# A Mamba block's weights for the scan prepared two steps earlier, and the next block's time-step work moved behind the first block's convolutions

## The chip, the cores and the metric

The kernel runs on one core of a Trainium2 chip. Its time is the device time of one launch in microseconds; a row of times comes from repeated launches, and one more launch is recorded by the hardware profiler. A core has a matrix engine (TensorE, PE in the profile), a vector engine (VectorE, DVE), a scalar engine (ScalarE, ACT) and GpSimd (POOL); SyncE (SP) issues most of the transfers. Each engine works through its own queue of instructions strictly in order, and a queue stands still while its first instruction waits for another engine.

## The reference

Four layers follow one another on an input of 2 x 1024 tokens of 512 features, each as `x = layernorm(x + layer(x))`: a Mamba-2 layer, a ternary linear layer, an RG-LRU layer and a gated feed-forward layer with integer weights. The change touches only the first. Cut to what matters:

```python
zxbcdt = hidden_states @ W_in                 # gate 1024 | x 1024, B 16, C 16 | dt 16
xBC = silu(causal_conv4(zxbcdt[..., 1024:2080]) + conv_b)
dt = softplus(zxbcdt[..., 2080:] + dt_bias)   # one per head, 16 heads of 64
dA = exp(dt * -exp(A_log))
# over the tokens t:
h = h * dA_t + (dt_t * x_t) outer B_t
y_t = h @ C_t
# then
y = (y + D_skip * x) * silu(gate)
y = y * rsqrt(mean(y * y) + 1e-5) * norm_w
out = y @ W_out
```

## The kernel before, in words

The 2048 tokens are worked on in four blocks (b = 0 to 3) of 512; two blocks make one sequence. Inside a block the recurrence over tokens is done in four chunks (c) of 128 tokens: the part inside a chunk is a product with a 128 x 128 matrix of weights for each head, and only the state H goes from chunk to chunk.

`head(b)` transposes the block's tokens (L219), multiplies them with the B, C and time-step columns of W_in (L340), convolves B and C (the taps at L251, 32 rows, silu at L299), and works out softplus and decays. For block 0 this is done on 128 partitions. For the others it is done in `by_rows`, on 64 rows of 128 tokens: L427 adds the bias, `softplus` (L195 to L206) follows, then L429 to L431, an exponential on ScalarE (L432), a cumulative product (L433), and two writes to DRAM (`since`, L436, and `decays`, L438). After a `yield` one transpose on TensorE (L442) and a copy (L443) bring the time steps and B into the layout `tk` by token.

`project(b)` runs for blocks 1 to 3. Four transfers (L546) broadcast the decays to all partitions of the tile L, 16 heads of 512 tokens, four heads each. Then eight steps m follow. `inner(m)` is a product of four matmuls into one PSUM bank (px, L323), a copy to SBUF (xpad, L458), the scaled start of the convolution (acc, L293), three taps on VectorE (L251) and a silu (xc, L299). `grams` makes the products of B and C (pgm, L474, copied to gm at L480). `scans(h0)` copies four heads of L into PSUM (pl, one bank each, L516) and makes running products of them on VectorE (L522). `weigh(h0)` makes bdec on VectorE (L532) and multiplies the four heads by gm on GpSimd (L537). `spans` fetches the decay since the start of a chunk (cdec, L493), with a small copy on VectorE (over, L505) and a product on GpSimd (L506). At the end `by_token` transposes the first chunk (pxt, L619) and scales it by the time steps (dtx, L621).

Between these steps `weave` puts pieces of `conclude(b - 1)`, the output product of the block before (po, L715, one bank for each of four groups of 128 tokens; the row sums pss, L724; the update of x, L730), by a plan that says after which step how many pieces come:

```python
            fill, plan = conclude(b - 1, before), (0, 0, 2, 0, 2, 0, 2, 2)
```

`recur(b)` is the recurrence: products py (L642 with the state, L650 within the chunk), the new state (pst, L660; L667, L674), the sum into xc (L681), and the next chunk's `by_token`. Between its chunks come pieces of `gates` (the gate's columns of W_in, pg, L323, silu at L692) and of the next block's `head`. Then `gate` multiplies by the gate on VectorE (L700), squares on ScalarE (L702) and adds up on GpSimd (L704).

Block 0 has no block before it. Its projection is written out in `opening`, where TensorE, VectorE and ScalarE keep the written order (`manual_schedule`); the convolutions there read PSUM (L306, taps L312, silu L316). Its last two lines before the remaining convolutions call the next block's head twice:

```python
        next(coming)
        for conv in later:
            next(g)
            conv()
```

The recurrence of block 0 then has the head of block 1 (`ahead`) and the gate (`g`) in turns:

```python
            turns = (ahead, g, g, ahead, g, g)
            weave(recur(b, H, st), (next(steps, None) for steps in turns), (2, 2, 1, 1))
```

Outside `opening` a planner that simulates the engines sets the order of the instructions in each queue; the program's order and its dependencies are what it starts from. `keep_in_program_order` pins an instruction to its place. The PSUM pool `ps` has eight banks with one tag, and all products share them in turn: a product must wait until the reader of an earlier tile in its bank is done.

Of the kernel before, what the change touches and what calls it, by code (L numbers as in the profile page):

```python
# [13 lines left out]
ALU = mybir.AluOpType  # L14
# [8 lines left out]
NX = DI // P  # L23
# [14 lines left out]
def model_kernel(ctx: ExitStack, tc: tile.TileContext, t: dict, out: bass.AP):  # L38
    nc = tc.nc
    ctx.enter_context(nc.allow_non_contiguous_dma(reason="small parameter columns"))  # L40
    BATCH, SEQ, _ = t["L0_attn_hidden_states"].shape
# [68 lines left out]
    by_hj = cp.tile([HJ, 5], F32, tag="by_hj", name="by_hj")  # L110
# [134 lines left out]
                x[:, j, :], x[:, j, :], mv[:, j, 0:1], rs[:, j, :], ALU.subtract, ALU.mult  # L245
            )

    def causal_conv(acc, xpad, w):

        for k in range(3):  # L250
            nc.vector.scalar_tensor_tensor(  # L251
                acc, xpad[:, k : k + TB], w[:, k : k + 1], acc, ALU.mult, ALU.add
            )

    def weave(main, fill, plan, rest=True):

# [29 lines left out]
    def started(pm, n, b, row, w, bias, dst, xpad):  # L286

        if b % BPS == 0:
            nc.gpsimd.memset(xpad[:n, 0:3], 0.0)
        else:  # L290
            nc.gpsimd.tensor_copy(xpad[:n, 0:3], carry[:n, row, :])
        acc = tmp("acc")
        nc.scalar.activation(acc[:n, :], pm[:n, :], AF.Identity, bias=bias, scale=w[:, 3:4])  # L293
        if b % BPS < BPS - 1:
            nc.gpsimd.tensor_copy(carry[:n, row, :], xpad[:n, TB : TB + 3])

        def rest():
            causal_conv(acc[:n, :], xpad[:n, :], w)
            nc.scalar.activation(dst, acc[:n, :], AF.Silu)  # L299

        return rest
# [27 lines left out]
    def head(b, st):  # L329

        if b >= 3:
            X.append(tokens())
            nc.sync.dma_start(X[b], xin[b])
        xT = st["xT"] = transposed(mp, b, X, bufs=2, by_act=b > 0)[0]

        pm = bank("pbc")
        half = TB // 2
        for k in range(NK):
            for i in range(2):
                nc.tensor.matmul(  # L340
                    pm[i * 64 : i * 64 + NR, :half], w_in[:, k, 2 * DI : IN_DIM],
                    xT[:, k, i * half : (i + 1) * half], start=(k == 0), stop=(k == NK - 1),
                )
        rows = mp.tile([P, 3 + TB], F32, tag="xpad", name="rpad", bufs=3)
        for i in range(2):
            nc.scalar.copy(
                rows[:NR, 3 + i * half : 3 + (i + 1) * half], pm[i * 64 : i * 64 + NR, :half]
            )
        BC = st["BC"] = mp.tile([NBC, TB], F32, tag="BC", name="BC")

        mix = started(rows[:, 3:], NBC, b, NX, cwr, cbr, BC, rows)
        tk = sp.tile([P, 2, NJ, NH], F32, tag="tk", name="tk")
        dt, bt = st["dt"], st["bt"] = tk[:, 0], tk[:, 1]
        if b:

            turn = mp.tile([P, P], F32, tag="a2", name="turn")
            nc.sync.dma_start(
                turn[:HJ], rows[32:NR, 3:].rearrange("h (j t) -> h j t", t=P)
            )
        if b < 2:  # L360
            yield
        if b:
            mix()
            nc.sync.dma_start(turn[HJ:], BC[:NS].rearrange("n (j t) -> n j t", t=P))
            nc.sync.dma_start(crow[b], BC[NS:])
            st["CT"] = mp.tile([P, TB], F32, tag="rows", name="CT", bufs=2)
            nc.sync.dma_start(st["CT"], crow[b].unsqueeze(0).to_broadcast([8, NS, TB]))
            yield
            yield from by_rows(b, turn, tk)
            return  # L370

        z = sp.tile([P, NJ, NH], F32, tag="z", name="z", bufs=1)
        a = sp.tile([P, NJ, NH], F32, tag="a", name="a", bufs=1)
        pdt = bank("pdt")
        for j in range(NJ):
            nc.tensor.transpose(
                pdt[:, j * NH : (j + 1) * NH], rows[32:NR, 3 + j * P : 3 + (j + 1) * P],
                ident[32:NR, 32:NR],
            )
        nc.vector.tensor_tensor(  # L380
            z, pdt[:, : NJ * NH].rearrange("p (j h) -> p j h", h=NH),
            dtb.unsqueeze(1).to_broadcast([P, NJ, NH]), ALU.add,
        )
        softplus(dt.rearrange("p j h -> p (j h)"), z.rearrange("p j h -> p (j h)"), NJ * NH)
        nc.vector.tensor_tensor(a, dt, rootA.unsqueeze(1).to_broadcast([P, NJ, NH]), ALU.mult)
        nc.vector.scalar_tensor_tensor(
            a, a, 1.0e18, rootN.unsqueeze(1).to_broadcast([P, NJ, NH]), ALU.min, ALU.mult
        )
        nc.vector.tensor_tensor(a, a, endless.unsqueeze(1).to_broadcast([P, NJ, NH]), ALU.min)
        for lo in (0, 32):  # L390
            nc.vector.tensor_scalar(a2[:, :, lo : lo + NH], a, LOG_FLOOR, None, ALU.max)
        yield
        pa = bank("pa")
        for j in range(NJ):
            nc.tensor.transpose(pa[:NR, j * P : (j + 1) * P], a2[:, j, :], ident)
        dA, cum = tmp("dA")[:NR], tmp("cum")[:NR]
        nc.scalar.activation(dA, pa[:NR, :], AF.Exp)

        r = st["r"] = mp.tile([NR, TB], F32R, tag="rows", name="rows", bufs=2)
        nc.scalar.activation(r, pa[:NR, :], AF.Exp)  # L400
        yield
        nc.vector.tensor_tensor(r[32:NR], dA[32:NR], r[32:NR].bitcast(F32), ALU.subtract)
        nc.vector.memset(r.bitcast(F32).rearrange("r (j t) -> r j t", t=P)[:, :, 0:1], 0.0)
        mix()
        yield
        for j in range(NJ):
            w = slice(j * P, (j + 1) * P)
            nc.vector.tensor_tensor_scan(
                cum[:, w], dA[:, w], zeros[:NR].to_broadcast([NR, P]), 1.0, ALU.mult, ALU.add
            )  # L410
        rc = st["rc"] = mp.tile([NR, TB], F32R, tag="rows", name="rows", bufs=2)
        nc.scalar.copy(rc, cum)
        yield
        nc.vector.tensor_tensor(rc[32:NR], cum[32:NR], rc[32:NR].bitcast(F32), ALU.subtract)
        yield

    def by_rows(b, turn, tk):


        z, work = turn[:HJ], [tmp(f"work{i}")[:HJ] for i in range(2)]  # L420
        e, r, s, s2, p, a, dA, cum = (
            w[:, i : i + P] for w in work for i in range(0, TB, P)
        )
        if b == 1:
            exponents(*(by_hj[:, i : i + 1] for i in range(1, 5)))
        bias, _, end, rA, rN = (by_hj[:, i : i + 1] for i in range(5))
        nc.vector.tensor_scalar(z, z, bias, None, ALU.add)  # L427
        softplus(z, z, P, (e, r, s, s2, p))
        nc.vector.tensor_scalar(a, z, rA, 1.0e18, ALU.mult, ALU.min)  # L429
        nc.vector.tensor_scalar(a, a, rN, end, ALU.mult, ALU.min)  # L430
        nc.vector.tensor_scalar(a, a, LOG_FLOOR, None, ALU.max)  # L431
        nc.scalar.activation(dA, a, AF.Exp)  # L432
        nc.vector.tensor_tensor_scan(  # L433
            cum, dA, zeros[:HJ].to_broadcast([HJ, P]), 1.0, ALU.mult, ALU.add
        )
        nc.sync.dma_start(since[b].rearrange("h (j t) -> (h j) t", t=P), cum)  # L436
        nc.vector.memset(dA[:, 0:1], 0.0)
        nc.sync.dma_start(decays[b].rearrange("h (j t) -> (h j) t", t=P), dA)  # L438
        yield

        pt = bank("ptk")
        nc.tensor.transpose(pt[:, :P], turn, ident)  # L442
        nc.vector.tensor_copy(tk, pt[:, :P].rearrange("p (v n j) -> p v j n", v=2, j=NJ))  # L443
        yield
# [96 lines left out]
    def project(b, st):  # L541

        inner, crows, grams, spans, scans, weigh = parts(b, st)

        for h0 in range(0, NH, 4):
            nc.sync.dma_start(  # L546
                L[:, h0 : h0 + 4, :].rearrange("p h t -> p (h t)"),
                decays[b, h0 : h0 + 4].rearrange("h t -> (h t)").partition_broadcast(P),
            )
        inner(0)()  # L550
        yield
        inner(1)()
        yield
        grams()
        inner(2)()
        yield
        for m in range(3, NX):
            inner(m)()
            if m == 6:
                spans()  # L560
            if m < 7:
                scans(4 * m - 12)
                weigh(4 * m - 12)
            yield
        st["dtx"] = by_token(st, 0)
        yield

    def opening(st, own, g, coming):
# [32 lines left out]
        later.pop(0)()  # L601
        later.append(inner(7))
        later.pop(0)()
        next(coming)
        for conv in later:
            next(g)
            conv()
# [140 lines left out]
    for b in range(NBLK):  # L748
# [5 lines left out]

            weave(recur(b, H, st), alternate(itertools.chain(fill, g), ahead), (3,) * NJ)
        else:
            turns = (ahead, g, g, ahead, g, g)
            weave(recur(b, H, st), (next(steps, None) for steps in turns), (2, 2, 1, 1))
            for m in range(NX):
                tc.keep_in_program_order(nc.gpsimd.tensor_scalar(  # L760
                    w_out[:, m, :], w_out[:, m, :], normw[:, m : m + 1], 1.0, ALU.mult, ALU.mult
# [492 lines left out]
```

## Time and profile before

| what | value |
|---|---|
| median of 3 runs | 1148.89 us (1146.79 to 1148.9) |
| time of the profiled execution | 1149.05 us |
| its span on the core | 1147.2 us |
| mean granted TensorE clock | 0.994 |
| TensorE / VectorE / ScalarE / GpSimd busy | 98% / 59% / 40% / 32% |
| block 0, projection | to about 72 us |
| block 0, recurrence | 72 to 106 us |
| blocks 1, 2, 3: projection starts | 106, 214, 319 us |
| last of block 3's recurrence | about 413 us |

The span runs from the first to the last instruction of the profiled execution, and lies 1.85 us under that execution's own time. Busy shares are means over the whole span, and the stages have different limits; so what a stage is worth is read from the waits inside it. A row of the timeline gives start, length, engine, line and tiles, and in brackets the idle time before it and what released it. A row of the waits gives who waited for whom, the sum in us, the count and the longest. In rows of windows each engine has its busy time, then comes the clock granted to TensorE (1.00 is full).

### The profile page before, as it was taken

To read this page: it belongs to the slowest core of one execution; us is meant where nothing else is said; L and a number is where in the kernel's file an instruction comes from. 1 tells how busy PE (TensorE), PEld (TensorE's weight loads), DVE (VectorE), ACT (ScalarE), POOL (GpSimd) and SP (SyncE) were. 2 spreads that over 40 slices of the span, in tenths; PEclk is the share of its full clock that TensorE was granted. 3 is DMA by queue.
4 is the path that set the end of the run, shared out by engine and by line. 5 is a ranking of instruction groups with operands and counts; after the bars stand their busy time and mean duration, and the time that the engine had idled before them with its cause. 6 is when DMAs were issued, how large, how long until landed. Compare 5 with 4: busy or idle time off the path is not lost.

```text
span 1147.2 us, 12259 instructions
## 1 busy us (share of the span) xinstructions
PE 1118.7 (98%) x4614; PEld 684.2 (60%) x4614; DVE 678.9 (59%) x1228; ACT 459.0 (40%) x700; POOL 361.9 (32%) x347
## 2 busy tenths in 40 slices
PE   8989999999999999999999999999999999999995
PEld 5455445445544555654444444448888888888884
DVE  4887896696769676863717237083328765225224
ACT  3343544463454233566654372533223223223222
POOL 1446472555248240556123212237401001001002
PEclk9999999999999999999999999999999999999998
DMA  8004002400220038112000000004501001001001
GB/s 316 20 14 167 2 1 89 166 0 37 69 113 0 38 144 234 74 31 89 1 1 0 1 0 1 0 1 128 175 1 38 1 1 37 1 1 37 1 1 40
DMA packets 32699, 59.22 MB, mean 52 GB/s; under 512 B 11808, under 2 KB 12608, under 8 KB 30072
## 3 DMA queue, kind: packets, MB, share of 16 engines
q1 hardware_dynamic: 31608, 58.21, 14.5%
q8 instruction: 38, 0.62, 0.2%
q14 instruction: 29, 0.24, 0.1%
q10 hardware_dynamic: 864, 0.14, 0.1%
q0 software_dynamic: 160, 0.01, 0.0%
HBM read 49.47 MB, written 8.68 MB: 51 GB/s over the span
## 4 chain that ended last, share of the span: by engine, by line
PE 84%; DVE 10%; ACT 4%; issue 1%; POOL 0%; DVEq 0%; ACTq 0%; POOLq 0%
PE pgu L1098 21%; PE p L947 17%; PE po L1121 10%; PE pg L323 9%; PE px L323 7%; PE po L715 6%; PE po L1024 4%; PE py L650 3%; DVE acc L251 2%; PE po L896 2%; DVE L L522 2%; PE pxt L619 1%; PE pt L219 1%; DVE xc L700 1%; PE py L642 1%
## 5 line engine op out<-in xcount | busy, mean ns | idle before, releaser
L1107 DVE SCALAR_TENSOR_TENSOR h<-pgu,L_ffn_up_scale,sg 128x512 f32<-128x512 f32 x64 | 47.9, 749 | 147.7 <-PE pgu L1098 143.7
L323 PE MATMUL px<-xT,w_in 128*128 128x512 f32 x256 | 114.6, 597 | 0.2 <-DVE over L509 0.2
L537 POOL TENSOR_TENSOR L<-L,gm 128x512 f32<-128x512 f32 x64 | 93.5, 1490 | 67.0 <-DVE bdec L532 29.4
L715 PE MATMUL po<-w_out,xc 128*128 128x512 f32 x256 | 112.5, 593 | 2.1 <-DVE L L522 2.1
L947 PE MATMUL p<-xT,w 128*128 128x512 f32 x256 | 112.1, 592 | 1.4 <-ACT xT L228 1.4
L323 PE MATMUL pg<-xT,w_in 128*128 128x512 f32 x256 | 113.4, 594 | 0.0
L947 PE MATMUL p<-cv,w 128*128 128x512 f32 x256 | 111.0, 592 | 0.0
L1121 PE MATMUL po<-wd,hh 128*128 128x512 f32 x256 | 101.3, 396 | 0.0
L1098 PE MATMUL pgu<-wF__4424,wg 128*128 128x512 f32 x256 | 101.2, 396 | 0.0
L1121 PE MATMUL po<-wd,hl 128*128 128x512 f32 x256 | 101.0, 394 | 0.0
L1098 PE MATMUL pgu<-lo__4425,wg 128*128 128x512 f32 x256 | 100.7, 393 | 0.0
L1098 PE MATMUL pgu<-lo__4425,wu 128*128 128x512 f32 x256 | 100.7, 393 | 0.0
L1098 PE MATMUL pgu<-wF__4424,wu 128*128 128x512 f32 x256 | 100.7, 393 | 0.0
L1105 ACT ACTIVATE sg<-pgu,L_ffn_gate_scale 128x512 f32<-128x512 f32 x64 | 44.0, 688 | 133.1 <-PE pgu L1098 133.0
L1113 ACT CAST hh<-h 128x512 fp32r<-128x512 f32 x64 | 39.7, 621 | 117.5 <-DVE h L1107 117.3
L715 PEld LDWEIGHTS po<-w_out,xc 128*128 128x128 f32 x256 | 48.4, 190 | 63.1 <-issue 55.7
L947 PEld LDWEIGHTS p<-cv,w 128*128 128x128 f32 x256 | 48.4, 190 | 59.8 <-issue 58.6
L947 PEld LDWEIGHTS p<-xT,w 128*128 128x128 f32 x256 | 48.4, 190 | 58.8 <-issue 55.3
L323 PEld LDWEIGHTS px<-xT,w_in 128*128 128x128 f32 x256 | 47.6, 190 | 57.8 <-issue 56.3
L1195 POOL TENSOR_TENSOR x<-x,r 128x512 f32<-128x512 f32 x12 | 15.2, 1294 | 205.9 <-DVE r L1194 205.9
L323 PEld LDWEIGHTS pg<-xT,w_in 128*128 128x128 f32 x256 | 47.4, 190 | 54.3 <-issue 53.7
L251 DVE SCALAR_TENSOR_TENSOR acc<-xpad,cols,acc 128x512 f32<-128x512 f32 x72 | 67.4, 939 | 18.5 <-ACT acc L293 14.8
(268 smaller groups left out, 1937.2 us busy)
## 6 DMA issues: line engine op xcount, KB each, us to landing
L<-decays SPq DMA_DIRECT2D x12, 1024.0 KB, 9.1
x_mid<-x SPq DMA_DIRECT2D x4, 1024.0 KB, 3.8
x<-x_mid SPq DMA_DIRECT2D x4, 1024.0 KB, 6.8
st<-in_L_ffn_gate_w_dram SPq DMA_DIRECT2D x8, 512.0 KB, 4.5
st<-in_L_ffn_up_w_dram SPq DMA_DIRECT2D x8, 512.0 KB, 4.1
st<-in_L_ffn_down_w_dram SPq DMA_DIRECT2D x8, 512.0 KB, 3.6
x<-_attn_hidden_states_dram SPq DMA_DIRECT2D x3, 1024.0 KB, 9.9
out_dram<-x SPq DMA_DIRECT2D x3, 1024.0 KB, 4.4
```

Of the source, the lines that this page charges most:

```text
L251: nc.vector.scalar_tensor_tensor(acc, xpad[:, k : k + TB], w[:, k : k + 1], acc, ALU.mult, ALU.add)
L323: nc.tensor.matmul(pm[:n, :], w_in[:, k, lo : lo + n], xT[:, k, :], start=(k == 0), stop=(k == NK - 1),)
L537: nc.gpsimd.tensor_tensor(L[:, h, :], L[:, h, :], st["gm"], ALU.mult)
L650: nc.tensor.matmul(pys[i][hh * HD : (hh + 1) * HD, q, :], dtx[q][:, 2 * i + hh, :], L[:, h, s], start=(first and q == 0), stop=(q == 1), s ...
L715: nc.tensor.matmul(po, xc[:, m, j * P : (j + 1) * P], w_out[:, m, :], start=(m == 0), stop=(m == NX - 1),)
L947: nc.tensor.matmul(pm, w1[:, i, k, m * P : (m + 1) * P], rhs[:, k, :], start=(k == 0), stop=(k == NK - 1),)
L1024: nc.tensor.matmul(po, y[:, k, j * P : (j + 1) * P], w1[:, 4, k, :], start=(k == 0), stop=(k == NK - 1),)
L1098: nc.tensor.matmul(pm, w[g][:, k, cols], x[:, k, :], start=(k == 0 and x is pieces[0]), stop=(k == NK - 1 and x is pieces[-1]),)
L1105: nc.scalar.activation(sg, pgu[0], AF.Silu, scale=gs[:, m : m + 1])
L1107: nc.vector.scalar_tensor_tensor(h, pgu[1], us[:, m : m + 1], sg, ALU.mult, ALU.mult)
L1113: nc.scalar.copy(hh, h)
L1121: nc.tensor.matmul(po[j], x[:, j * P : (j + 1) * P], wd[m // GK][:, m % GK, :], start=(m == 0 and x is h[0]), stop=(m == NF - 1 and x is h ...
```

## The change

In `project`, the steps for blocks 1 to 3: `grams` stands right behind `inner(0)` (before: behind `inner(1)`), `scans` and `weigh` of the four groups of heads stand at steps 1 to 4 (before: 3 to 6), and `spans` at step 5 (before: 6). The output product's pieces keep their places in the plan.

In `opening`, the second call of the next block's head is gone, so that the convolution of block 1's B and C comes in the recurrence of block 0. The turns of that recurrence are now head, gate, head, gate, gate, gate, head, with two pieces behind the first two chunks, one behind the third and two behind the last. Two instructions are pinned for block 1: the first of the three taps of B and C, and the addition of the bias that starts the softplus, which now also stands ahead of `exponents`.

```diff
-    def causal_conv(acc, xpad, w):
+    def causal_conv(acc, xpad, w, pinned=False):
 
         for k in range(3):
-            nc.vector.scalar_tensor_tensor(
+            tap = nc.vector.scalar_tensor_tensor(
                 acc, xpad[:, k : k + TB], w[:, k : k + 1], acc, ALU.mult, ALU.add
             )
+            if pinned and k == 0:
+                tc.keep_in_program_order(tap)
...
-        def rest():
-            causal_conv(acc[:n, :], xpad[:n, :], w)
+        def rest(pinned=False):
+            causal_conv(acc[:n, :], xpad[:n, :], w, pinned)
             nc.scalar.activation(dst, acc[:n, :], AF.Silu)
...
-            mix()
+
+            mix(b == 1)
...
+        bias, _, end, rA, rN = (by_hj[:, i : i + 1] for i in range(5))
+        shifted = nc.vector.tensor_scalar(z, z, bias, None, ALU.add)
         if b == 1:
+
+            tc.keep_in_program_order(shifted)
             exponents(*(by_hj[:, i : i + 1] for i in range(1, 5)))
-        bias, _, end, rA, rN = (by_hj[:, i : i + 1] for i in range(5))
-        nc.vector.tensor_scalar(z, z, bias, None, ALU.add)
...
         inner(0)()
+        grams()
         yield
-        inner(1)()
-        yield
-        grams()
-        inner(2)()
-        yield
-        for m in range(3, NX):
+        for m in range(1, NX):
             inner(m)()
-            if m == 6:
+            if m == 5:
                 spans()
-            if m < 7:
-                scans(4 * m - 12)
-                weigh(4 * m - 12)
+            if m < 5:
+                scans(4 * m - 4)
+                weigh(4 * m - 4)
             yield
...
-        next(coming)
         for conv in later:
             next(g)
...
-            turns = (ahead, g, g, ahead, g, g)
-            weave(recur(b, H, st), (next(steps, None) for steps in turns), (2, 2, 1, 1))
+            turns = (ahead, g, ahead, g, g, g, ahead)
+            weave(recur(b, H, st), (next(steps, None) for steps in turns), (2, 2, 1, 2))
```

## The prediction

> **What bounds the kernel now.** I read the page's first part, then TensorE's waits between 50 and 425 us (the Mamba layer, the only part that the diff touches), its clock, and the order of time on VectorE and TensorE in the blocks.
>
> ```profile
> PE 1118.7 (98%) x4614; PEld 684.2 (60%) x4614; DVE 678.9 (59%) x1228; ACT 459.0 (40%) x700; POOL 361.9 (32%) x347
> ```
>
> TensorE is busy 98% of the span. A busy TensorE is no proof of its peak, but it means that time is won or lost only where TensorE stands still or runs at a lower clock. The list of waits, as waiting line, released by, us in total, times, longest:
>
> ```profile
> PE pxt L619 <- ACT xc L316: 2.4, 1, 2.4
> PE po L715 <- DVE L L522: 2.1, 2, 1.1
> PE py L650 <- issue: 0.8, 2, 0.6
> PE pxt L619 <- ACT xc L299: 0.7, 1, 0.7
> PE pt L219 <- DVE L L522: 0.5, 1, 0.5
> ```
>
> So the layer holds 6.5 us of standing still. The first wait also has an after-effect; here is TensorE's clock behind it (time, then busy of each engine, then the granted clock):
>
> ```profile
> 71.50:72.50 1.00, 0.98 (x8) 0.69 (x6) 1.00 (x3) 0.60 (x1) 0.20 (x1) 1.00 0.15 33
> ...
> 76.00:77.00 1.00, 1.00 (x12) 1.00 (x9) 0.73 (x2) 0.00 (x0) 0.37 (x1) 0.50 0.00 0
> ```
>
> The reader is to see 0.50: from about 75.5 to 78.8 us the clock is halved. Here is what it costs (start, length, TensorE's pieces of block 0's first and second chunk):
>
> ```profile
> 75.18 3.41 PE L650 MATMUL py<-L,dtx 128*64 128x128 f32 x32
> 78.52 0.84 PE L660 MATMUL pst<-dtx,bdec 128*32 128x128 f32 x16
> ...
> 84.40 1.97 PE L650 MATMUL py<-L,dtx 128*64 128x128 f32 x32
> 86.30 0.65 PE L660 MATMUL pst<-dtx,bdec 128*32 128x128 f32 x16
> ```
>
> The same work takes 1.44 + 0.19 us more the first time; with the transposes between, 1.7 us. Last, VectorE and TensorE in block 2, where the change has its second place:
>
> ```profile
> 219.33 3.57 DVE L251 SCALAR_TENSOR_TENSOR acc<-xpad,cols,acc 128x512 f32<-128x512 f32 x3 [1.91 <-ACT acc L293]
> ...
> 224.39 2.33 DVE L251 SCALAR_TENSOR_TENSOR acc<-xpad,cols,acc 128x512 f32<-128x512 f32 x3 [1.41 <-POOL cdec L506]
> ...
> 232.15 1.22 DVE L522 TENSOR_TENSOR_SCAN L<-pl,id 128x512 f32<-128x512 f32 x1 [1.18 <-ACT pl L516]
> ```
>
> ```profile
> 225.23 7.03 PE L715 MATMUL po<-w_out,xc 128*128 128x512 f32 x16
> ...
> 239.86 1.45 PE L715 MATMUL po<-w_out,xc 128*128 128x512 f32 x3
> ```
>
> VectorE has idle time early in a projection stage and scans late; TensorE reaches the first output product (po, j = 0) at 225.23 and the second at 239.86 without a wait. Blocks 2 and 3 have next to nothing to win.
>
> **The change, part by part.** No instruction is added or removed; by the built orders everything is moved, and PSUM banks, taken in program order, go to other pairs of tiles.
>
> (a) *Block 0's end.* Taken out of VectorE's queue ahead of the last convolution: three 32-row taps (L251), L427, L195, L197, L198, L199. ScalarE no longer puts two table loads (1.28 each) and two activations there. From 65.17 two convolutions of three L312 taps at 0.67 to 0.76 = 2 x 2.14 end at 69.45 (before: 74.07). ScalarE's silu of the last one then stands behind the gate's silu, which waits for TensorE and ends at 72.35; so it ends at 72.98, not 74.87. The last transpose moves from 74.92 to 73.03: **1.9 us**. The clock: TensorE did only transposes and waiting from 71.55 to 75.18, and the drop follows at 75.5; now that stretch is 71.55 to 73.3. The Trainium skill (TensorE: Matmul & The Clock Gate, Part 1) puts the drop behind an idle free-running window of about 3.4 us, and Part 4 says that transposes don't count as busy the same way; 3.6 us agrees with that, 1.75 stays below it. I take the clock as kept: **1.7 us**. Sum 3.6.
>
> (b) *Where that work goes.* The three taps go behind the second chunk's dtx, where VectorE waits for TensorE: free. The chain from L427 to the first L203 (3.1 us in block 2: 189.73 to 192.84) starts behind the last dtx of chunk 2, near 87.0, so the first L203 ends at 90.4. Then five more L203, L204, L206, L429 (0.3 each) alternate with the L681, L667, L674 and L621 of that chunk. The last L621 (dtx) ends at 96.3 to 97.1, TensorE wants it at 96.35: between 0 and 0.8, I take **0.4 lost**. Queued behind the decay's exponential and L433 and L437 are block 0's last L681 and the whole gate: they start at 98.2 (100.46 before), so VectorE gains 2.25 where TensorE gains 3.2. SyncE's loads of L wait for the decays, written at about 99 and landed 1.8 later; issued at 101.3, the first lands 5.5 to 6.3 behind that (what blocks 3 and 2 show), about 107, which ScalarE asks for at 113.5: hidden. What is left of the transposed tk (L442, L443) costs 0.2 and 0.15.
>
> (c) *Scans at steps 1 to 4: what is late next.* In the new order the first po waits for the bank of the **third scan**, and the second po for that of the **eleventh**. Behind them TensorE's whole in-order queue waits.
> Block 1: the gate, at VectorE's own pace (113.18 - 2.26 + 0.15), ends at 111.1. As before 1.9 us of ScalarE follow to the first tap (sq, xpad, acc): 113.0. Two taps beside GpSimd at 1.34 and 1.0 (1.34 and 1.65 before): 115.35. Scan, tap, scan, scan = 1.14 + 0.65 + 2 x 1.14: 119.4. TensorE gets there at 102.55 + 0.2 + px 3.43 + pgm 1.08 + px, px 6.87 = 114.1. Wait: **5.3 us**, where before there was none.
> Block 2: taps from 219.33 to 222.1, plus 4.07 gives 226.2; TensorE wants 225.2 (pgm only trades places with px): **1.0**. Block 3: taps 323.73 to 326.73, 330.85 against 330.4: **0.5**.
> From the third scan to the eleventh VectorE has 8 scans x 1.14, 6 taps x 0.65, 2 bdec x 0.33, over and reciprocal 0.15 each, L730 0.72 = 14.7, and waits 0.8 for ScalarE (a silu 0.63 stands ahead of the copy to pl, 0.55) and 0.4 for the rms behind its table load (a 0.35 of that kind is in the trace at 129.79): 15.9. TensorE needs 14.6 (225.23 to 239.86). So each second po waits **1.3**, in three blocks.
> What block 1 waits for now goes: 1.05 + 1.01 (po) and 0.65 (pxt): the last taps come at 160.7 to 163, po ends at 166: **2.7 won**.
>
> (d) *Clock in the new gap.* By the row alone (a gap of 2.44 us with transposes was enough) 5.3 us of standing still drops the clock surely: 1.7. By the skill's rule a free-running window of 3.4 must lie wholly inside: (5.3 - 3.4)/3.4 = 56%, so 0.95. I take **1.0**, ends 0 and 1.7.
>
> Sum: -3.6 + 0.4 - 2.7 = -5.9; block 1 5.3 + 1.3 + 1.0, block 2 1.0 + 1.3, block 3 0.5 + 1.3 = +11.7. Net **+5.8 us**. The profiled execution took 1149.05 (span 1147.2), the median of the runs shown is 1148.89, the same but for 0.2; so 1149.05 + 5.8 = 1154.85, against the median 1154.7. Everything behind the first layer keeps its order and shifts as a whole.
>
> **Rivals.**
> *The scans keep up (other side).* Place: block 1's first po. If its third scan ended by 114.1, and the second po and blocks 2 and 3 waited for nothing, the 5.9 won would stand: 1143.0. It decides at 11.7 new us falling under 5.9 - 2.3. For it: before, VectorE idles 1.8 + 1.5 + 1.9 + 1.2 us between 113 and 130, room that the scans could fill. Against: the 1.9 of ScalarE, two taps and three scans are 8.3 us in sequence behind the gate, and TensorE arrives 3 us behind it.
> *About no change.* The clock holds, taps run alone at 0.65 to 0.73 (1.0 less before each first po), and each second po waits 0.3: losses 4.3 + 0.3, 0 + 0.3, 0 + 0.3 against 5.9: 0.7 under the median, 1148.2. For it: the scan, which reads PSUM, kept 1.2 us everywhere. Against: the taps at 115 and 324 us, in the same place, took 1.34 and 1.5.
> *GpSimd takes VectorE's time.* Its weighing (L537, 1.26 to 1.8 each) now begins while taps of one convolution follow each other; beside GpSimd a tap took 1.34 to 1.65. Six taps per block at +0.5 make each second po 3 us later: 5.8 + 9 gives 1164. Against: alternating with scans (135 to 142 us) taps took 0.72 with GpSimd busy.
> *It does not do what it says*: ScalarE's gate silu holds the last xc, and the first wait and half clock stay: 1154.7 + 3.6 less what block 1's wait shrinks by, nothing or up to 3.6: 1155 to 1158.
>
> **How the numbers follow.** A measurement of this kernel tells 0.2% (2.3 us) from no change. Chances: forecast 0.62 (1151.5 to 1158.5, by the ends: 4 us lower if no clock drop, no dtx stall and one second po in time, 4 us higher if the taps or L674 are slowed), the scans keep up 0.06, about no change 0.14, GpSimd 0.08, no effect at block 0 0.10. Faster 0.07 (the scans keep up, a corner of the next); same 0.13; slower 0.80. For 8 in 10 the range leaves out 1143 and the tail of 1164: 1149 to 1159.
>
> **What would show it.** Right: no wait of pxt on L316 above 0.8 and no 0.50 clock near 76 us; po waiting for L522 six times, the longest about 5 us near 114, three near 1.3; no pxt wait on L299. Wrong: the first po starting within 1 us of px's end in block 1, or po waiting for something other than a scan. If po waits for more than 2 us in blocks 2 and 3 each, taps beside GpSimd were dearer than I took them. A half clock behind the long gap shows (d).

## The result, and the profile after

The changed kernel takes 1153.59 us (median of 6 runs, 1152.64 to 1156.67), the kernel before 1148.57 us beside it (6 runs, 1146.52 to 1150.29). The ratio is 1.0047, with a 95% interval of 1.0031 to 1.0063: slower by half a per cent. The profiled execution took 1153.5 us with a span of 1151.3 us; before it was 1149.05 and 1147.2.

The page's first part for the changed kernel has nearly the same busy time on TensorE, VectorE 8 us less, GpSimd 3 us more:

```profile
PE 1119.2 (97%) x4614; PEld 682.1 (59%) x4614; DVE 671.1 (58%) x1228; ACT 458.8 (40%) x700; POOL 364.6 (32%) x347
```

TensorE's waits in the Mamba layer of the changed kernel (waiting line, released by, us in total, times, longest):

```profile
PE po L715 <- DVE L L527: 4.4, 5, 1.1
PE po L715 <- POOL sums L704: 2.1, 1, 2.1
PE py L650 <- issue: 1.0, 3, 0.6
PE py L650 <- DVE dtx L621: 1.0, 2, 0.8
PE pt L219 <- DVE L L527: 0.5, 1, 0.5
PE pxt L619 <- ACT xc L318: 0.4, 1, 0.4
```

The 2.4 us of pxt behind the silu (now L318) have become 0.4, and the 0.7 us behind L299 are gone. In their place po waits six times, 6.5 us together, where it waited twice for 2.1. The second row names GpSimd's sums, which ended at the same moment; by the program's dependencies this po waits for the bank that the third scan (L527) reads, and only the pss behind it needs the sums. The times agree: each of the six po's starts 0.10 to 0.15 us after the end of a third or an eleventh scan.

The six waits, one by one, in the timeline of TensorE (the bracket is the idle time ahead):

```profile
118.82 1.53 PE L715 MATMUL po<-w_out,xc 128*128 128x512 f32 x3 [2.14 <-POOL sums L704]
...
134.77 5.82 PE L715 MATMUL po<-w_out,xc 128*128 128x512 f32 x13 [1.08 <-DVE L L527]
...
226.05 4.53 PE L715 MATMUL po<-w_out,xc 128*128 128x512 f32 x10 [0.88 <-DVE L L527]
...
241.96 7.11 PE L715 MATMUL po<-w_out,xc 128*128 128x512 f32 x16 [1.04 <-DVE L L527]
...
333.11 7.10 PE L715 MATMUL po<-w_out,xc 128*128 128x512 f32 x16 [0.40 <-DVE L L527]
...
349.01 1.53 PE L715 MATMUL po<-w_out,xc 128*128 128x512 f32 x3 [1.04 <-DVE L L527]
```

They stand at the first and the second po of each block. In the later two blocks nothing was won that could pay for them.

TensorE's first and second chunk of block 0, to be set against the 3.41 and 0.84 of before:

```profile
74.52 2.26 PE L650 MATMUL py<-L,dtx 128*64 128x128 f32 x32
76.71 0.65 PE L660 MATMUL pst<-dtx,bdec 128*32 128x128 f32 x16
...
82.40 1.97 PE L650 MATMUL py<-L,dtx 128*64 128x128 f32 x32
84.30 0.64 PE L660 MATMUL pst<-dtx,bdec 128*32 128x128 f32 x16
```

The half clock at 76 us is gone. Another one is in this execution, earlier, in work that the change doesn't touch (39.4 to 42.8 us). Windows of 4 us (time, then busy of each engine, then the granted clock):

```profile
36.00:40.00 4.00, 4.00 (x21) 2.48 (x19) 2.58 (x8) 1.93 (x4) 0.00 (x0) 0.92 0.00 0
40.00:44.00 4.00, 4.00 (x7) 1.75 (x7) 3.93 (x6) 0.63 (x1) 3.63 (x3) 0.65 0.00 0
...
76.00:80.00 4.00, 4.00 (x42) 2.67 (x38) 3.85 (x8) 0.00 (x0) 1.98 (x2) 1.00 0.00 0
```

It costs 1.34 us: block 0's last px starts that much later than before. How far the changed kernel is behind the other at some points of TensorE's queue (start after minus start before, us) shows where the time went:

| point | behind by | step |
|---|---|---|
| last px of block 0 | +1.34 | +1.34, half clock near 40 us |
| py of chunk 0 | -0.66 | -2.00, pxt's wait |
| first pxt behind it | -2.01 | -1.35, full clock in py and pst |
| pg of chunk 3 | -0.87 | +1.14, wait for dtx |
| first px of block 1 | -0.77 | +0.10 |
| first po of block 1 | +1.54 | +2.31, third scan |
| second po | +1.65 | +0.11, 1.08 in place of 1.05 |
| third po | +0.44 | -1.21, old wait gone |
| block 1's first py | -0.53 | -0.97, old wait of pxt gone |
| first px of block 2 | -0.23 | +0.30 |
| first and second po of block 2 | +0.82, +2.10 | +1.05 and +1.28 |
| first px of block 3 | +2.17 | +0.07 |
| first and second po of block 3 | +2.74, +4.01 | +0.57 and +1.27 |
| last po of block 3 | +4.09 | +0.08 |

The last row is the difference of the spans (1151.3 - 1147.2). A restart behind a wait costs 0.1 to 0.3 us beyond the wait itself.

### The profile page after: what moved, and what is told of

The parts are those of the page before. It is cut to its first block, busy times and chain, and to the rows that moved or that the text cites. A ratio compares the mean times of both kernels' runs of the same rounds, so it can differ in the third digit from the quotient of the medians.

```text
span 1151.3 us, 12249 instructions
## 1 busy us (share of the span) xinstructions
PE 1119.2 (97%) x4614; PEld 682.1 (59%) x4614; DVE 671.1 (58%) x1228; ACT 458.8 (40%) x700; POOL 364.6 (32%) x347
## 4 chain that ended last, share of the span: by engine, by line
PE 81%; DVE 12%; ACT 4%; issue 2%; DMA 1%; POOL 0%; DVEq 0%; ACTq 0%; POOLq 0%
PE pgu L1098 21%; PE p L947 17%; PE po L1121 10%; PE pg L325 8%; PE po L715 7%; PE px L325 6%; PE po L1024 4%; DVE L L527 3%; PE py L650 2%; PE po L896 2%; DVE acc L251 2%; DVE xc L700 1%; PE pxt L619 1%; PE pt L219 1%; PE py L642 1%
## 5 line engine op out<-in xcount | busy, mean ns | idle before, releaser
L1113 ACT CAST hh<-h 128x512 fp32r<-128x512 f32 x64 | 39.7, 621 | 117.6 <-DVE h L1107 117.4
L527 DVE TENSOR_TENSOR_SCAN L<-pl,id 128x512 f32<-128x512 f32 x64 | 75.4, 1209 | 4.8 <-PE pl L523 2.6
```

The source lines that it names most:

```text
L527: nc.vector.tensor_tensor_scan(L[:, h, :], pl, id4.rearrange("p j t -> p (j t)"), 0.0, ALU.mult, ALU.add)
L1113: nc.scalar.copy(hh, h)
```

## The experiments

Theory 1: the change is two changes that pull against each other. Block 1's B, C and time-step work, moved, wins at the end of block 0; the earlier scans lose, because po takes over a PSUM bank from a scan that isn't done. Theory 2: VectorE's work itself is too much at the start of a projection, or the moved work makes it late, whatever bank is asked for.

### Only the moved rows

```diff
# against the changed kernel
         inner(0)()
-        grams()
         yield
-        for m in range(1, NX):
+        inner(1)()
+        yield
+        grams()
+        inner(2)()
+        yield
+        for m in range(3, NX):
             inner(m)()
-            if m == 5:
+            if m == 6:
                 spans()
-            if m < 5:
-                scans(4 * m - 4)
-                weigh(4 * m - 4)
+            if m < 7:
+                scans(4 * m - 12)
+                weigh(4 * m - 12)
             yield
```

> Only block 1's B, C and time-step work is moved behind the taps; the order of Grams and scans is that of before. Theory 1 (the two halves of the change pull against each other, and the loss is the PSUM bank that po takes over from a scan): the first pxt wait of block 0 falls from 2.4 to about 0.4 us (2.0 won), the half clock behind it is gone (1.7 won), dtx ahead of chunk 3 costs 0.95; block 1 keeps its old waits of about 1 us on the first late po and on pxt. Sum -2.7: about 1145.9 us, 0.2% faster than before. If one half-clock stretch falls somewhere in the layer in every execution, the 1.7 is not won: about 1147.5. Theory 2 (the moved work itself is what makes the change slow, through VectorE's lateness at the end of block 0): slower than before, 1150 or more, with waits on dtx or on xc of over 2 us in block 1.

Measured: 1147.25 us (21 runs) against 1149.18 (41 runs), ratio 0.9988 (0.9981 to 0.9994): faster by 0.1%. Its waits (po is at L719 here, pxt at L623, py at L654):

```profile
PE po L719 <- DVE L L527: 1.9, 2, 1.0
PE py L654 <- DVE dtx L625: 0.9, 2, 0.8
...
PE pxt L623 <- ACT xc L301: 0.7, 1, 0.7
...
PE pxt L623 <- DVE dtx L625: 0.4, 1, 0.4
```

pxt's first wait is 0.4, dtx costs 0.9 and block 1 keeps its old waits, as theory 1 had it. The profile has a half clock at 36 to 44 us again (0.93 and 0.64), and that execution took 1148.52 us, not the 1147.5 given for that case. Thirteen of the 21 runs lie at 1146.8 to 1147.4 with a mean clock of 0.996 or 0.997, so most likely without it; 1145.9 was given for them. The best runs of the kernel before are no slower (4 of 41 at 1146.6 to 1146.9). So part of the 0.1% is probably that half-clock stretches come in fewer runs, and what the shorter wait gave by itself is not settled. This half of the change is by its median a small win, and no loss; theory 2's second form falls.

### Only the earlier Grams and scans

```diff
# against the kernel before: project() as in the change
         inner(0)()
+        grams()
         yield
-        inner(1)()
-        yield
-        grams()
-        inner(2)()
-        yield
-        for m in range(3, NX):
+        for m in range(1, NX):
...
-            if m < 7:
-                scans(4 * m - 12)
-                weigh(4 * m - 12)
+            if m < 5:
+                scans(4 * m - 4)
+                weigh(4 * m - 4)
```

> Only the Grams and scans are earlier; block 1's B, C and time-step work stays where it was before. Theory 1: the gate of block 0 ends at about 113.2, the third scan at about 122, TensorE wants the first po of block 1 near 117.5: a wait of 4 to 5 us there on the bank of L522's third scan, then 1.1, 0.9, 1.0, 0.4, 1.0 at the later po's as in the changed kernel; the old 2.7 us of waits in block 1 go. Sum +6: about 1154.5 us. Theory 2 (the moved work is what costs): about as before, 1147 to 1150.

Measured: 1157.95 us (5 runs, 1155.12 to 1158.54), ratio 1.0076 (1.0062 to 1.0089). The first po of block 1 in the timeline, and the clock behind it in windows of 4 us:

```profile
120.34 8.80 PE L711 MATMUL po<-w_out,xc 128*128 128x512 f32 x16 [5.03 <-DVE L L522]
```

```profile
116.00:120.00 4.00, 0.00 (x0) 0.00 (x0) 4.00 (x5) 2.07 (x4) 0.23 (x2) 1.00 0.00 0
120.00:124.00 4.00, 3.66 (x5) 1.65 (x6) 4.00 (x7) 2.94 (x6) 1.69 (x2) 0.58 0.01 2
```

The wait is 5.03 us, and behind it the clock is halved: this po takes 8.80 where the later ones take 7.1, 1.7 us more. Theory 1's sum had the wait right and left out the clock; the profiled execution took 1155.12 us with a mean clock of 0.995, the other four 1156.84 to 1158.54 with 0.992, so they probably hold more half clock; where, no trace shows. The sums of GpSimd were done here 4.8 us before this po started, and it still waited for the scan. So the loss is in the scans' new place, and the moved rows take part of it back: alone it costs 8.8 us by the medians, together with the rows 5.0.

### No PSUM bank for the scans

```diff
# against the changed kernel
             for h in range(h0, h0 + 4):
-                pl = bank("pl")
                 if b:
-                    nc.scalar.copy(pl, L[:, h, :])
+                    pl = L[:, h, :]
                 else:
+                    pl = bank("pl")
                     nc.tensor.matmul(
```

> The changed kernel, but for blocks 1 to 3 the scan reads the decays where they lie in SBUF: no PSUM bank pl and no ScalarE copy into it, so po never takes over a bank from a scan. Theory 1 (the bank is what makes TensorE wait): all six waits of po on L527 go (2.1 + 1.1 + 0.9 + 1.0 + 0.4 + 1.0 = 6.5 us), and no wait above 0.7 us takes their place: about 1147 us. Theory 2 (VectorE has too much to do in a projection stage, and the bank only shows where): the lateness comes back as waits of pxt on xc, of py on L or of po on the end of VectorE's queue, and the time stays at 1152 to 1154. A scan that reads SBUF beside GpSimd could also be dearer than its 1.15 us from PSUM; that would show in its own rows.

Measured: 1191.64 us, ratio 1.0375 (1.036 to 1.0389). No po waits for a scan any more, but far longer waits stand at pxt. TensorE's waits, two rows of VectorE's timeline, and one of GpSimd's:

```profile
PE pxt L619 <- ACT xc L301: 22.9, 7, 3.9
PE pxt L619 <- DVE x L730: 7.9, 2, 4.2
PE px L325 <- ACT rms L728: 4.5, 2, 3.7
```

```profile
109.08 8.72 DVE L527 TENSOR_TENSOR_SCAN L<-L,id 128x512 f32<-128x512 f32 x4
...
129.64 2.31 DVE L527 TENSOR_TENSOR_SCAN L<-L,id 128x512 f32<-128x512 f32 x2
```

```profile
133.06 4.40 POOL L542 TENSOR_TENSOR L<-L,gm 128x512 f32<-128x512 f32 x2 [3.37 <-issue]
```

A scan that reads both inputs from SBUF takes 1.2 us while GpSimd is idle (the two from 129.64 us on) and mostly 2.2 beside a GpSimd product (the four from 109.08 on); from PSUM all 48 took 1.19 to 1.22. A few of the 1.21 stand beside a GpSimd product too, and then the product is the one that takes longer (2.72 us for the first of the two from 133.06 on). The 48 scans of blocks 1 to 3 take 1.97 on the mean, 36 us more than at 1.21, and VectorE becomes the bound. So the run doesn't tell the theories apart: it took the bank away and made the scans 1.6 times as long on the way. It shows what the copy into PSUM is for.

### Scans and weighing one step later

```diff
# against the changed kernel
-            if m < 5:
-                scans(4 * m - 4)
-                weigh(4 * m - 4)
+            if 2 <= m < 6:
+                scans(4 * m - 8)
+                weigh(4 * m - 8)
```

> The changed kernel with the Grams still right behind the first inner product, but scans and weighing at steps 2 to 5 instead of 1 to 4. By the order of the banks the first po of a block then waits for no scan, the second for the seventh scan (not the eleventh), the third for the twelfth, the fourth for the thirteenth. Theory 1: in block 1 the seventh scan ends near 128, and TensorE wants the second po near 131: no waits at the first two po's, 6.5 us less than the changed kernel, about 1147 us. Theory 2 (VectorE's amount of work is the limit): the waits move to the third or fourth po or to pxt, each over 1 us, and the time stays above 1151.

Measured: 1147.95 us (21 runs), ratio to before 0.9985 (0.9979 to 0.9992). One wait for a scan is left in the three blocks:

```profile
PE po L715 <- DVE L L527: 2.0, 1, 2.0
PE py L650 <- issue: 1.0, 3, 0.6
PE py L650 <- DVE dtx L621: 0.9, 2, 0.8
```

VectorE has the same instructions to do, so its amount of work is not what makes TensorE wait: one step in the program's order gives back 5.6 us of medians. A miss is in it: the seventh scan was put near 128 us and ended near 135 in an execution with half clock from 38.9 to 45.8, and the second po of block 1 waited 2.0 us for it.

### The same scans, another bank for po

```diff
# against the changed kernel
+    spare = []
...
+            if b and m in (2, 4):
+                j = m // 2 - 1
+                spare.append(bank("po"))
+                nc.tensor.matmul(
+                    spare[0], before["xc"][:, 0, j * P : (j + 1) * P], w_out[:, 0, :],
+                    start=True, stop=False,
+                )
             if m < 5:
                 scans(4 * m - 4)
...
-            po = bank("po")
-            for m in range(NX):
+            begun = len(spare)
+            po = spare.pop() if begun else bank("po")
+            for m in range(begun, NX):
```

> The changed kernel, but in blocks 1 to 3 the first matmul of po for j = 0 and 1 is written ahead of that step's scans in the program. TensorE's order stays as it was; only the bank that po gets is another (for the first po that of px of step 0, for the second that of the ninth scan instead of the eleventh), and in blocks 1 to 3 a few scans trade places with taps. Theory 1 (the loss is the wait for the bank): no wait at the first po's, 0 to 1 us at the second ones; of the six waits (6.5 us) at least 5.5 are gone: about 1147.5 us. Theory 2 (VectorE's lateness, whatever the bank): the same 2 us come back at the next thing that TensorE wants of VectorE in block 1 (pxt on xc, py on L), and at least 1 us per block in blocks 2 and 3: 1151 or more.

Measured: 1153.87 us, ratio to before 1.0037 (1.0023 to 1.005): nothing won against the changed kernel. No po waits; a px does, behind the first po, its pss and one px more. The waits of the run, and the place in block 1:

```profile
PE px L325 <- DVE L L527: 7.4, 3, 3.0
```

```profile
122.83 3.68 PE L325 MATMUL px<-xT,w_in 128*128 128x512 f32 x8
129.49 1.78 PE L325 MATMUL px<-xT,w_in 128*128 128x512 f32 x3 [2.98 <-DVE L L527]
```

Theory 1 falls in the form it had. Which tile asks for the bank didn't matter here: eight banks go round, four scans of a step take four of them, and whatever TensorE starts next but a few (po, px, pss) comes to a bank that a scan still reads. In each block the new wait is about as long as the two that it replaces, or longer: 2.98 for 3.22, 1.87 for 1.92, 2.52 for 1.44. Behind the 2.98 and the 2.52 the clock is halved too, which no wait of the changed kernel brought about; it costs about 1.7 and 1.5 us in the profiled execution (1155.38). Theory 2 had the time, 1151 or more, but not the place: neither pxt nor py waits more. Together with the run before this leaves as the likely account: the loss is how far the scans are put ahead of TensorE's products in that round, before VectorE has caught up.

### The time-step chain one chunk later

```diff
# against the run with another bank for po
-            turns = (ahead, g, ahead, g, g, g, ahead)
-            weave(recur(b, H, st), (next(steps, None) for steps in turns), (2, 2, 1, 2))
+            turns = (ahead, g, g, ahead, g, g, ahead)
+            weave(recur(b, H, st), (next(steps, None) for steps in turns), (2, 1, 2, 2))
```

> As the last, and the time-step chain of block 1 (L427 and what follows it) goes into VectorE's queue behind the third dtx of block 0's recurrence, one chunk later than in the changed kernel. Theory 1, with the wait for dtx put down to the chain's pieces in front of it: the 0.95 us of py waiting for dtx go; the decays are written some 3 us later, so the loads of L land near 112 instead of 109, as late as ScalarE wants them, but the first po no longer needs a scan: about 1146.5 us, 0.2% under before. Against: if the late loads make scans late, the second po of block 1 waits by 1 to 3 us, and the time is 1147.5 to 1149.

Measured: 1158.68 us, ratio to before 1.0083 (1.0069 to 1.0097), a clear miss. TensorE's waits:

```profile
PE px L325 <- DVE L L527: 4.4, 2, 2.5
PE pss L734 <- DVE L L527: 4.2, 1, 4.2
...
PE ptk L447 <- PE pg L325: 0.9, 1, 0.9
```

The 0.95 at dtx are gone, and 0.95 come back at ptk in the same recurrence. Then ScalarE's squares (L711) wait for GpSimd's sums, which now take 2.04 us each; block 1's first tap starts at 113.76 us where it was 110.55, the first scan at 122.50 where it was 113.26, and pss waits 4.24 us. Behind that wait the clock is halved for 6.83 us, which costs another 3.4. It is one more case of a small shift ahead of block 1 that comes out larger at the scans. What part each of the late decays and the slowed sums has in it was not tried.

### Both kernels once more

> The kernel before, once more, for where its half-clock stretch falls. If the drop at 75.5 us belongs to the 2.4 us gap, it is there again. If the window in which TensorE's activity is counted runs freely, it can be missing there, and one may lie near 36 to 44 us (behind the stretch of narrow matmuls L474, L476), as in the changed kernel's profile.

> The changed kernel, once more. If the half clock at 36 to 44 us is chance, it can be missing; then TensorE comes to the first po of block 1 about 1.3 us earlier, the third scan is no earlier, and the wait is about 3.5 us instead of 2.1.

Measured: 1149.05 and 1152.34 us in the profiled executions. Windows of 4 us, first of the kernel before, then of the changed one:

```profile
40.00:44.00 4.00, 4.00 (x10) 1.81 (x10) 3.93 (x6) 1.03 (x2) 3.77 (x4) 1.00 0.00 0
...
76.00:80.00 4.00, 4.00 (x48) 3.47 (x46) 2.80 (x8) 0.00 (x0) 0.34 (x2) 0.68 0.00 0
```

```profile
40.00:44.00 4.00, 4.00 (x10) 1.85 (x11) 3.93 (x6) 0.86 (x2) 3.60 (x3) 1.00 0.00 0
...
76.00:80.00 4.00, 4.00 (x16) 2.18 (x16) 3.83 (x6) 0.00 (x0) 2.04 (x2) 1.00 0.00 0
```

The kernel before has its half clock behind pxt's 2.44 us again. The changed kernel has none at all this time, at 40 us neither: that one differs from launch to launch. The second expectation failed in its last part: the first po of block 1 started 1.36 us earlier (117.46 in place of 118.82), and the third scan ended as much earlier; the wait stayed at 2.15. VectorE follows TensorE through block 0's recurrence, so an early delay moves both and cancels there.

### Scans at steps 2, 4, 5 and 6

```diff
# against the changed kernel
-            if m == 5:
+            if m == 6:
                 spans()
-            if m < 5:
-                scans(4 * m - 4)
-                weigh(4 * m - 4)
+            if m in (2, 4, 5, 6):
+                h0 = 4 * (m - 3) if m > 2 else 0
+                scans(h0)
+                weigh(h0)
```

> Block 1's B, C and time-step work as in the changed kernel, Grams behind the first inner product, scans and weighing at steps 2, 4, 5 and 6. By the order of the banks the first po of a block waits for no scan, the second only for the pss that rms is read from, the third for the eleventh scan (as in the kernel before, but VectorE has done four scans in the idle time that it had ahead of 127 us). Theory now (what costs is that TensorE takes a bank from a scan before VectorE has caught up with the gate; the number of scans between is what counts, not which tile waits): the waits of 0.85, 1.01 and 0.65 us in block 1 of the run with only the rows moved go too, dtx's 0.95 stays: about 1145 us, 0.3% faster than before. Rival (VectorE is full between 110 and 160 us whatever the order): the same 2 to 2.5 us wait in block 1, on the third po or pxt, about 1147.3 us.

Measured: 1146.11 us (22 runs) against 1148.74 (27 runs), ratio 0.998 (0.9972 to 0.9988): it beats both kernels, the changed one by about 7.5 us. Its best runs are better too (1145.07 us against 1146.73). Its waits in the layer, all of 0.4 us and more:

```profile
PE py L651 <- DVE dtx L622: 0.9, 2, 0.8
PE py L651 <- issue: 0.8, 2, 0.6
PE pxt L620 <- ACT xc L301: 0.6, 1, 0.6
PE po L716 <- DVE L L527: 0.5, 1, 0.5
PE pt L219 <- DVE L L527: 0.5, 1, 0.5
PE pxt L620 <- DVE dtx L622: 0.4, 1, 0.4
```

Four scans go into time in which VectorE had been idle, and no bank of theirs comes up soon. po waits 0.5 us where the rows alone had 1.9; the 0.6 of pxt stay, against the theory, so by the medians it is 1.1 us less than with the rows alone, not 2.5. The rival, 2 to 2.5 us on whatever comes, doesn't stand.

## Why the prediction was right

The forecast was 1154.7 us, the measured median 1153.6. Most steps held by place. Four were off in size: the first po of block 1 and the clock behind it, 6.3 us together, came to 2.3 in the table; the stall at dtx and the half clock behind pxt came out worse than forecast, by 0.7 and 0.35. That the sum came as near as it did is in part luck: the profiled execution also had the 1.34 us of half clock at 40 us, which was not forecast. In the second pair of profiles, without it, the spans are 2.8 us apart. Direction and range didn't need the luck, as that execution took 1152.34 us.

**(a) Block 0's end.** 1.9 us were forecast for pxt and 2.0 measured. For the clock 1.7 were forecast; py and pst of the first chunk got 1.34 us shorter. The term was mis-sized because the second chunk's 1.97 us of py stood for full clock, while the first chunk takes 2.26 at full clock. The stretch itself belonged to the gap: in two profiles of before it follows the 2.44 us; in the nine others, where this gap is 0.44 or 1.57, it is not there.

**(b) Where that work goes.** 0.4 us at dtx were forecast, with 0.8 as the worst; measured 0.17 + 0.78 = 0.95, and 1.14 with the restarts. Two L203 at 0.79 and 0.78, an L674 at 0.77 and an L434 at 0.69 stand in front of the two dtx while GpSimd runs L625 and L760. The three narrow ones are 1.4 us over the 0.28 that the same rows take ahead of it, more than the whole wait; the forecast had 0.3 for each. Not all were slowed: L204 and L206 kept 0.27.

**(c) The first po of block 1.** This is the step that failed by size: 5.3 us forecast, 2.14 and 2.15 measured. The third scan ended at 117.4 us in the second profile (no half clock ahead), not 119.4, and TensorE came at 115.3, not 114.1. TensorE's part is dtx (0.55 more) and restarts. VectorE's part is the gate, taken over from before with its own pace (12.7 us) and measured at 9.2. Before, the last six L700 took 9.05 us; two rows of VectorE's timeline of the changed kernel, then GpSimd's row of the same stretch:

```profile
104.15 2.49 DVE L700 TENSOR_TENSOR xc<-xc,g 128x512 f32<-128x512 f32 x4
...
106.76 3.23 DVE L700 TENSOR_TENSOR xc<-xc,g 128x512 f32<-128x512 f32 x2
```

```profile
104.52 11.30 POOL L704 TENSOR_TENSOR sums<-sums,sq 128x512 f32<-128x512 f32 x6 [3.37 <-ACT sq L702]
```

Four of the six ran at 0.62 us in place of 1.5, and GpSimd's sums at 1.9 in place of 1.63. In the second profile the gate started 1.2 us later than forecast (99.4) and ended 2.5 earlier (108.6). The two taps behind it took 1.4 each, not 1.34 and 1.0. With the gate as before, in the run of only the scans (six L700 in 9.06 us there), the wait was 5.03. So the sum was right for the gate's old pace, and that the moved rows change this pace was not foreseen.

**(c) The other waits.** Second po's: 1.3 three times forecast, 1.08, 1.04 and 1.04 measured. First po's of blocks 2 and 3: 1.0 and 0.5 forecast, 0.88 and 0.40 measured. Old waits of block 1: 2.7 won, as forecast. The working behind these (taps and scans in sequence behind the last wait of VectorE) was right in kind and, within 0.3 us, in size.

**(d) Clock in the new gap.** 1.0 us forecast, nothing paid, since the gap stayed at 2.15. That a gap of five can cost it is shown by the run of only the scans (5.03 us, then 0.58 of the clock, 1.7 us). The rule behind the 56% was too mild: a whole window of 3.4 us needn't lie inside the gap, as 2.2 to 3.1 us of one did (last section).

The mechanism that the prediction gave, the bank that the third and the eleventh scan hold, is what the trace shows, but it is not a property of po: moved to another bank, the wait went to px. Of its signs, the six waits came, but the longest was 2.1 us near 117 and not 5 near 114. Of the rivals, none came: the scans did not keep up, and the dearer taps of "GpSimd takes VectorE's time" came to 0.05 and 0.4 us for the two in block 1. That the two halves go opposite ways was the net of the sum, and the two runs with one half each confirm it.

## What to carry to other kernels

In a pool whose banks go round, moving work earlier in the program also moves its banks earlier in the round: count for each product of the bounding engine whose reader it must wait for, and work out when that reader is done at the start of a stage, where its engine is late, not on the mean. If the wait is found, another tile for the bank moves it on; another distance between the two (here one or two steps) removes it. And split a change that has two parts: here one part was worth 0.1% by the median, and put together with a milder form of the other 0.2%.

## What the runs showed of the hardware

**Two SBUF inputs beside GpSimd.** A scan with both inputs in SBUF goes from 1.21 to 2.2 us beside GpSimd, a tap from 0.65 to 1.65, each by about 1.0; GpSimd's product L625 takes 1.04. A scan with one input in PSUM doesn't change. The Trainium skill (SBUF — State Buffer, SBUF: two separate sides) describes the port that VectorE and GpSimd share as an exclusive lock for a whole instruction, taken by whichever starts first, and the rows agree with whole instructions. Not expected was that the loser isn't fixed: in the same code, on the same tiles, VectorE and GpSimd took turns before (1.75 and 1.6 us each), while after it VectorE ran four L700 in 2.49 us and GpSimd took 4.93 for two. It goes with the kernel and not with the launch: three profiles with the rows in their old place have the first pattern, seven with the rows moved have the second (the late chain orders this part otherwise). What decides it was not found; both begin with VectorE some 0.36 us ahead.

**Where the half clock falls.** In these profiles every half-clock stretch before the program's end lasts 3.41 us, or two, four or five times that, and the stretches of full clock between them are whole multiples too (64.85 us before, 19 times). So the clock is set anew every 3.41 us, on a grid that starts at another moment in each launch: the free-running window of the prediction. What counts is how long TensorE stands still inside one cell of this grid. Two waits of the same px in block 3 show it: 2.52 us from 343.49 on in the run with another bank, 2.51 us from 346.67 on in the run with the late chain. Here is for each the cell with most of the wait in it, and the cell behind (time, then busy of each engine, then the granted clock):

```profile
342.31:345.72 3.41, 1.18 (x3) 0.19 (x1) 3.41 (x4) 0.96 (x2) 0.09 (x1) 1.00 0.00 0
345.72:349.13 3.41, 3.13 (x4) 1.51 (x5) 3.24 (x6) 3.38 (x7) 2.68 (x3) 0.50 0.00 0
```

```profile
345.00:348.41 3.41, 1.67 (x4) 0.38 (x2) 3.41 (x5) 0.47 (x1) 0.58 (x1) 1.00 0.00 0
348.41:351.82 3.41, 2.64 (x6) 1.25 (x7) 3.24 (x6) 3.38 (x7) 2.19 (x2) 1.00 0.00 0
```

The first wait lies in one cell for 2.23 us and the clock is halved behind it. The second is cut by an edge into 1.74 and 0.77 us, and the clock stays. In the Mamba layer of the eleven profiles, of the cells at full clock all with 1.2 to 2.02 us of standing still kept it behind them, and all with 2.19 or more lost it. The 2.44 us before lay in one cell in both profiles; the 2.15 of the changed kernel put 2.02 us into one cell in the second profile, and was cut in two by an edge in the first. It isn't standing still alone, though: at the end of the program before, a cell with 1.97 us lost it. A stretch of 3.41 us cost 1.3 to 1.7 us, one of 6.83 us 3.4.

In three of the eleven profiles a half clock begins at about 39 us, where TensorE has no wait over 0.2 us, behind a stretch of narrow matmuls (L479 and L481, 0.48 and 0.17 us for two and one, from 36.4 us on). In these three the edge of a cell lies at 38.94, 39.37 and 39.47 us, in the other eight at 37.62 to 38.82. So the place of the grid sorts the launches; that the narrow matmuls are what is counted as low is argued, not shown. The run times fit: those of before lie in groups near 1147, 1149 and 1150.6 us, and its two profiles, with one stretch each, took 1149.05; those of the last kernel lie near 1145.3 and 1147, and its profile, with none, took 1145.47.
